# A two-layer transformer on one core: one more slot before layer 0's last mixing, sums at the ends of slots from there on, and a last block stored tile by tile

## The chip, the cores and the metric

The kernel runs on 1 core of a Trainium2 chip. The metric is the device time of one execution in microseconds (us). All matrix work is float32.

TensorE (PE) multiplies; its weight loads are shown as PEld. VectorE (DVE), ScalarE (ACT) and GpSimd (POOL) do the elementwise work, and SyncE (SP) issues nearly all DMAs. "PEclk" is the TensorE clock that was granted, as a share of full speed.

## The reference

The input `x` has 4 sequences of 512 positions with 256 features. Two transformer layers follow, each an attention and a feed-forward part behind a layer norm without parameters, with a residual add:

```
x = x + L0_attn(layernorm(x))   # 16 heads of 16, causal, softmax over up to 512 keys
x = x + L0_ffn(layernorm(x))    # per token AND output feature: softmax over 8 experts, the best two mixed
x = x + L1_attn(layernorm(x))   # 16 query heads of 128 on 4 key heads; attention over the 4 batch entries only
x = x + L1_ffn(layernorm(x))    # gated GELU, 256 -> 2048 -> 256, weights in 4 bits with scales
```

The feed-forward part of layer 0 is the one whose order matters here. For a token it computes 8 x 256 router logits and 8 x 256 expert results; for each of the 256 output features the two greatest of 8 logits choose two experts, their softmax weights are computed, all weights of one expert are summed over the 256 features, and the sums `c` (8 per token) mix the 8 expert results:

```
logits = (h @ router_w.T + router_b).reshape(T, O, E)
probs = softmax(logits); w, sel = top_k(probs, 2); w = w / sum(w)
c = zeros((T, E)).at[t_idx, sel].add(w)          # summed over the O features
final = einsum('te,teo->to', c, einsum('th,eoh->teo', h, expert_w) + expert_b)
```

## The kernel before

The 2048 tokens are 16 groups of 128 (the partitions), in 4 blocks of 4 groups. The residual stream `xres` stays in SBUF throughout. The order of instructions on PE, DVE, ACT and GpSimd is the order of the program, written out by hand.

**Layer 0's attention** is a loop over 44 batches `n` (block `j`, sequence `s`, head groups `gs`). A step issues the scores of the next batch (`greatest`, L652), subtracts this batch's maxima from the queries (`shift`, L681 and L684), adds the causal mask (`mask`, L665) and takes maxima (L671). Then follow a first `fill`, `mixed(n - 1)` (L736, the values times the exponentials, and their copy `avs`, L744), `powers(n)` (L700, the scores again; ACT's exponentials L709 into `pt`; GpSimd's causal zeroing L719) and a second `fill`. After the loop `mixed(43)` closes the layer.

**Slots.** `fill` is one slot of filler work. It counts `slot` up, gives PE and DVE a budget in us (what was overdrawn is carried over), and lets every `Stream` in `streams`, in order, emit its next piece while its engine has budget left and its condition holds. Streams are generators that yield `need(engine, cost, gap, cond)` before each piece; `gap` is a number of slots since the stream's piece before. The streams that matter here:

- `logit_pieces` (`lg`) and `result_pieces` (`eo`), the *products*: per group 4 router and 4 expert products of four matmuls each (L234), price 1.85. A product of logits needs the weights of two groups before; an expert product needs its group's weights, and its halves wait for earlier additions. ACT copies a logits product (L297), and multiplies an expert product by its two weights (L323, `part`).
- `weight_pieces`: DVE finds the two greatest of 8 (L371 to L397). ACT computes the lesser weight's tanh (`lesser`, L390, L391), two slots later. Then for each of 8 experts DVE writes a tile `owing` (L408, L426) and sums one part (L423), while ACT sums the other part from `owing` into `sums` (`sum_up`, L415). `total_pieces` (L436, L437) finishes the weights once all 8 sums are emitted.
- `addition_pieces` (L350 to L352): DVE adds four `part` tiles into `xres`.
- `divided(j, s)`: after a sequence's last mixing PE transposes `avs` (`av_T`, L754), DVE divides (L761, L762, `oq`), PE transposes back (`oq_T`, L771, only in an odd slot) and ACT copies that to `aT` (L774). After the last sequence of a block PE multiplies by `wo` in two steps (`o`, L783), each added to `xres` by DVE a slot or more later (L793).
- `norm_pieces`: a layer norm in pieces (statistics L180 and L181, `rs_v` L184, GpSimd's power L185, `xn` L194).

What `weight_pieces` hands to ACT isn't emitted at once. `defer(emit, slots, last)` puts it off by a slot (or two), and `emit_deferred` issues it either at the start of the slot where it is due, ahead of all streams, or at its end. For `sum_up` that is now decided by the slot in which it is put off:

```python
                defer(sum_up, last=slot % 2 == 1)
                yield need("DVE", 0.95, cond=lambda: len(deferred) < 6)
```

The PSUM pool `dn` has two tiles, which the products, `av_T`, `oq_T`, `o` and most projections take in turn.

**Layer 1's attention** loops over 16 head groups `p` (plus a first step for the projections of group 0): projections L987, scores L1000, softmax on DVE, values L1058, output L1078. Between its pieces `between` calls `fill` nine times a group, and what is left of layer 0's products is spread over the groups up to `LAST = 8`:

```python
            share = products_left / (9 * (LAST + 1 - p)) if p <= LAST else 0.0
```

with a PE budget of `1.9 * share + 0.2` and a DVE budget of `2.7 * share + 1.4` a slot. At `p == LAST + 2` a loop empties whatever is left before the last layer's weights are unpacked on DVE. Block 3's norm and transposes (`start_pieces(3)`) need the last addition of group 15 and must be done when `p == 11` begins.

**Layer 1's feed-forward part** computes gate and up (L916), the GELU on ACT and DVE, and `down` (L1234, `y`): per group 16 matmuls, then DVE's add into `xres` (L222). After the fourth group of a block one DMA on SP stores the block (L1239).

Of the kernel before, what the change touches and what calls it, by code (L numbers as in the profile page):

```python
# [21 lines left out]
NBLK = 4  # L22
# [10 lines left out]
def tile_transformer(  # L33
# [19 lines left out]
    nc = tc.nc  # L53
# [4 lines left out]
    xres = const.tile([P, NT, HID], F32, name="xres")  # L58

    def load_x(j):  # L60
        nc.sync.dma_start(
            out=xres[:, 4 * j : 4 * j + 4, :], in_=x[:, 4 * j : 4 * j + 4, :]
        )
# [48 lines left out]
    slot = 0  # L112

    def need(engine, cost, gap=0, cond=None):
        return engine, cost, gap, cond
# [21 lines left out]
    def defer(emit, slots=1, last=False):  # L137


        deferred.append((slot + slots, emit, last))  # L140

    def emit_deferred(last):
        for due in [d for d in deferred if d[0] <= slot and d[2] == last]:
            deferred.remove(due)
            due[1]()

    left = {"PE": 0.0, "DVE": 0.0}

    def fill(**budget):

        nonlocal slot
        slot += 1
        emit_deferred(False)
        for engine, b in budget.items():
            left[engine] = min(left[engine], 0.0) + b
        again = True
        while again:
            again = False
            for stream in list(streams):
                while stream.ready(left):  # L160
                    engine, cost = stream.go()
                    left[engine] -= cost
                    again = True
                if stream.next is None:
                    streams.remove(stream)
        emit_deferred(True)
# [188 lines left out]
    def weight_pieces():  # L355

        tt, stt = nc.vector.tensor_tensor, nc.vector.scalar_tensor_tensor
        lessers = []
        for g in range(NT):
            yield need("DVE", 1.25, cond=lambda: g in logits and logits[g][1] < slot)  # L360
            d = logits[g][0]
            hi4 = b1.tile([P, 4, HID], F32, tag="hi4", name=f"hi4_{g}")
            lo4 = b1.tile([P, 4, HID], F32, tag="lo4", name=f"lo4_{g}")
            m2 = b1.tile([P, HID], F32, tag="m2", name=f"m2_{g}")
            gap = b1.tile([P, HID], F32, tag="gap", name=f"gap_{g}")
            th = b1.tile([P, HID], F32, tag="th", name=f"th_{g}")
            w1 = b1.tile([P, HID], F32, tag="w1", name=f"w1_{g}")
            c1 = b5.tile([P, NE], F32, tag="c1", name=f"c1_{g}")
            sums = b5.tile([P, NE + 1], F32, tag="sums", name=f"sums_{g}")

            tt(hi4, d[:, 0:4], d[:, 4:8], ALU.max)  # L371
            yield need("DVE", 1.25)
            tt(lo4, d[:, 0:4], d[:, 4:8], ALU.min)
            yield need("DVE", 1.4)
            lo2, hi2 = lo4[:, 0:2], lo4[:, 2:4]
            tt(lo2, lo2, lo4[:, 2:4], ALU.max)
            tt(hi2, hi4[:, 0:2], hi4[:, 2:4], ALU.max)
            yield need("DVE", 1.4)
            tt(hi4[:, 0:2], hi4[:, 0:2], hi4[:, 2:4], ALU.min)
            tt(lo2, lo2, hi4[:, 0:2], ALU.max)  # L380
            yield need("DVE", 1.7)
            tt(gap, hi2[:, 0], hi2[:, 1], ALU.min)
            tt(m2, lo2[:, 0], lo2[:, 1], ALU.max)
            tt(m2, m2, gap, ALU.max)
            tt(gap, hi2[:, 0], hi2[:, 1], ALU.max)
            tt(gap, gap, m2, ALU.subtract)


            def lesser(th=th, gap=gap, w1=w1):
                nc.scalar.activation(th, gap, AF.Tanh, scale=0.5)  # L390
                nc.scalar.activation(w1, th, AF.Identity, bias=half_t, scale=0.5)  # L391
                lessers.append(th)

            defer(lesser, 2)
            for e in (0, 4):
                yield need("DVE", 1.25)
                tt(  # L397
                    d[:, e : e + 4], d[:, e : e + 4],
                    m2.unsqueeze(1).to_broadcast([P, 4, HID]), ALU.subtract,
                )  # L400

            yield need("DVE", 0.7, 1, cond=lambda: lessers)
            lessers.clear()
            owing = b5.tile([P, HID], F32, tag="owing", name=f"owing_{g}_")
            nc.vector.tensor_scalar(gap, gap, 0.0, -1.0, ALU.is_equal, ALU.mult)
            stt(owing, th, -1.0, gap, ALU.add, ALU.add)  # L408
            nc.vector.memset(sums[:, NE : NE + 1], 0.0)
            summed_up[g] = [c1, sums, 0]  # L410
            for e in range(NE):

                def sum_up(e=e, owing=owing, sums=sums, g=g):
                    spare = b2.tile([P, HID], BF16, tag="spare", name=f"spare_{g}_{e}")
                    nc.scalar.activation(  # L415
                        spare, owing, AF.Relu, scale=-1.0, accum_out=sums[:, e : e + 1]
                    )
                    summed_up[g][2] += 1

                defer(sum_up, last=slot % 2 == 1)  # L420
                yield need("DVE", 0.95, cond=lambda: len(deferred) < 6)
                junk = b2.tile([P, HID], BF16, tag="junk", name=f"junk_{g}_{e}")
                stt(junk, d[:, e], 0.0, w1, ALU.is_gt, ALU.mult, accum_out=c1[:, e : e + 1])  # L423
                if e < NE - 1:
                    less = b5.tile([P, HID], F32, tag="owing", name=f"owing_{g}_{e}")
                    stt(less, d[:, e], 0.0, owing, ALU.is_equal, ALU.add)  # L426
                    owing = less
            del logits[g]
# [20 lines left out]
    with ExitStack() as l0:  # L449
# [20 lines left out]
        def blank(j, i):  # L470
# [22 lines left out]
            out=later, in_=later, compare_op=ALU.is_ge, fill=NEG,  # L493
# [140 lines left out]
        for j in range(NBLK):  # L634
            n = (4, 2, 1, 1)[j]
            for s in range(NS):
                batches += [(j, s, range(g, g + n)) for g in range(0, 4, n)]
        NBT = len(batches)
# [194 lines left out]
        for n in range(NBT):  # L833
            j, s, gs = batches[n]
            if n in (1, 7):
                to = 2 if n == 1 else 3
                inputs[to] = Stream(prepare(to))
                streams.insert(0, inputs[to])
            if n + 1 < NBT and batches[n + 1][0] != j:
                while inputs[j + 1].next is not None:  # L840
                    fill(PE=2.0, DVE=2.0)
            with tc.high_priority(offset=AHEAD):
                if n + 1 < NBT:
                    greatest(n + 1)
                shift(n)
                if n + 1 < NBT:
                    mask(n + 1)

            fill(PE=(2.0, 2.0, 1.8, 1.6)[j], DVE=2.6)
            with tc.high_priority(offset=AHEAD):  # L850
                if n:
                    mixed(n - 1)
                powers(n)
            done += 1
            if n and batches[n - 1][2][-1] == 3:
                streams.insert(0, Stream(divided(*batches[n - 1][:2])))
            fill(PE=(2.4, 2.4, 2.2, 2.0)[j], DVE=2.6)
            if n < 4:
                w, dram = (rw, router_w) if n < 2 else (ew, expert_w)
                for i in range(4):  # L860
                    load_pair(w, dram, 4 * n % 8 + i)
                    loaded[n // 2, (4 * n % 8 + i) // 2] = slot
            for _ in range(1 + (n < 2) if blanked < 10 else 0):
                blank(2 + blanked // 5, (blanked + 4) % 5)
                blanked += 1
            if n in (0, 2):
                load_x(n // 2 + 2)
        mixed(NBT - 1)
        streams.insert(0, Stream(norm_pieces(0, b1, b2, normed_first)))
        last = Stream(divided(*batches[NBT - 1][:2]))  # L870
# [56 lines left out]
    with ExitStack() as l1:  # L927
# [3 lines left out]
        for kv, i in [(slice(None), slice(HPK + 1, HPK + 2))] + [  # L931
            (slice(kv, kv + 1), slice(0, HPK + 1)) for kv in range(NKV)
        ]:
            for hc in range(2):
                tc.keep_in_program_order(
                    nc.sync.dma_start(
                        out=wqkv[:, hc, kv, i], in_=w_qkv[hc * P : (hc + 1) * P, kv, i]
# [188 lines left out]
        for p in range(-1, NP):  # L1126
            j, kv = divmod(p, NKV)
# [54 lines left out]
    with ExitStack() as f1:  # L1182
# [47 lines left out]
        def down(j, it):  # L1230
            for t in range(4):
                ps = ps_o.tile([P, HID], F32, tag="o", name=f"y_{j}_{t}")
                for c in range(2 * NJ):
                    nc.tensor.matmul(  # L1234
                        ps, lhsT=it[:, c // 2, c % 2, t * P : (t + 1) * P],
                        rhs=wd[:, c // 2, c % 2, :], start=c == 0, stop=c == 2 * NJ - 1,
                    )
                add_residual(4 * j + t, ps)
            nc.sync.dma_start(  # L1239
                out=out[:, 4 * j : 4 * j + 4, :], in_=xres[:, 4 * j : 4 * j + 4, :]  # L1240
            )

        pending = None
        for j in range(NBLK):
# [62 lines left out]
```

## Time and profile before

| | |
|---|---|
| median of 3 runs | 1169.55 us (1169.44 to 1170.32) |
| the profiled execution | 1170.3 us, span 1168.6 us |
| granted TensorE clock in it | 1.000 |
| PE busy | 1142.0 us, 98% of the span |
| DVE busy | 809.8 us, 69% |
| ACT busy | 484.3 us, 41% |
| GpSimd busy | 108.4 us, 9% |
| waits of PE from 365 to 400 us (end of layer 0) | 4.1 us |
| waits of PE from 400 to 720 us (layer 1's attention beside layer 0's products) | 3.3 us |
| last store: issue | 1164.98 us |

The span runs from the first to the last instruction of one profiled execution; the time of an execution holds some more around it. Rows of the order of time read: start, duration, engine, line, operation, what is written from what, how many, and in brackets how long the engine had stood idle before and what released it. Rows of waits read: who waited for whom, the total, the times and the longest, in us. Rows by stretch read: the stretch and its length, then busy time and number of instructions of PE, PEld, DVE, ACT and POOL, the granted clock, the DMA engines' busy share and GB/s. Rows of DMA issues read: transfer, issuing queue, number, size of one and median us from issue to landing.

### The profile page before, as it was taken

Reading aid. Unit: us, or ns where it says so; the run is one execution under the profiler, and the core shown is the slowest. Engines: PE = TensorE matmul, PEld = TensorE weight load, DVE = VectorE, ACT = ScalarE, POOL = GpSimd, SP = SyncE. Lnnn points to the kernel's source line nnn. Section 1 sums busy time; section 2 is a strip of 40 time slices with the busy share of each in tenths; the row PEclk is TensorE's granted clock in tenths of the full one; section 3 lists DMA queues with packets and bytes.
Section 4 is the critical chain, followed back from the end, with each engine's and each line's share of the span. In section 5 each row is a group of like instructions: output and inputs, shape, how many; then the busy total and the mean of one; then the engine's idle time right before and its main releaser. Section 6 shows DMA issues by size and latency. Waiting matters only on the chain.

```text
span 1168.6 us, 18563 instructions
## 1 busy us (share of the span) xinstructions
PE 1142.0 (98%) x7178; PEld 661.5 (57%) x7178; DVE 809.8 (69%) x1783; ACT 484.3 (41%) x1099; POOL 108.4 (9%) x152
## 2 busy tenths in 40 slices
PE   7999999999999999999999999999999999999998
PEld 3666555556554445555555555566644475484487
DVE  5676889999988953868773785687699845716710
ACT  1444645556555542444443444544344312303300
POOL 7322221212112000000000000000000000000000
PEclk9999999999999999999999999999999999999999
DMA  7230110000000500000000001120110000000000
GB/s 219 64 83 2 19 20 2 2 1 2 2 2 1 181 1 1 1 1 1 1 1 1 1 1 46 28 54 21 27 46 1 0 1 19 0 1 19 1 18 19
DMA packets 21239, 26.46 MB, mean 23 GB/s; under 512 B 5128, under 2 KB 14600, under 8 KB 21152
## 3 DMA queue, kind: packets, MB, share of 16 engines
q1 hardware_dynamic: 20480, 24.10, 7.5%
q10 hardware_dynamic: 672, 1.18, 0.4%
q8 instruction: 56, 0.92, 0.3%
q14 instruction: 31, 0.25, 0.1%
HBM read 18.97 MB, written 2.10 MB: 18 GB/s over the span
## 4 chain that ended last, share of the span: by engine, by line
PE 81%; DVE 13%; ACT 2%; issue 1%; POOL 1%; DMA 0%; SPq 0%; ACTq 0%; DVEq 0%; POOLq 0%
PE qk_ps L987 11%; PE y L1234 9%; PE o L1078 9%; PE g L916 9%; PE u L916 9%; PE lg_ps L234 8%; PE eo L234 7%; PE s L652 3%; PE s L700 3%; DVE mx L671 3%; PE av L736 2%; PE v_ps L969 2%; PE qk_ps L545 2%; PE a L1058 1%; PE s L1000 1%
## 5 line engine op out<-in xcount | busy, mean ns | idle before, releaser
L987 PE MATMUL qk_ps<-xT,wqkv 128*128 128x512 f32 x320 | 148.9, 599 | 2.3 <-ACT part L323 1.2
L234 PE MATMUL lg_ps<-rw,xT 128*128 128x512 f32 x256 | 122.5, 601 | 1.4 <-ACT xT L954 0.3
L234 PE MATMUL eo<-ew,xT 128*128 128x512 f32 x256 | 121.5, 600 | 0.8 <-ACT lg L297 0.5
L1078 PE MATMUL o<-wpj,oT 128*128 128x256 f32 x512 | 119.1, 382 | 0.0
L1234 PE MATMUL y<-wd,it 128*128 128x256 f32 x512 | 111.8, 379 | 0.0
L1078 PEld LDWEIGHTS o<-wpj,oT 128*128 128x128 f32 x512 | 95.9, 190 | 27.5 <-issue 14.3
L1234 PEld LDWEIGHTS y<-wd,it 128*128 128x128 f32 x512 | 97.0, 190 | 15.0 <-issue 2.2
L671 DVE TENSOR_REDUCE mx<-s 128x1 f32<-128x384 f32 (+3 forms) x176 | 100.4, 632 | 1.3 <-PE s L665 1.3
L987 PEld LDWEIGHTS qk_ps<-xT,wqkv 128*128 128x128 f32 x320 | 59.1, 190 | 71.4 <-issue 57.4
L709 ACT ACTIVATE pt<-s 128x512 f32<-128x512 f32 (+1 forms) x176 | 84.1, 563 | 35.3 <-PE s L700 35.3
L916 PE MATMUL g<-xT,wgu 128*128 128x512 f32 x192 | 90.4, 593 | 0.0
L916 PE MATMUL u<-xT,wgu 128*128 128x512 f32 x192 | 90.2, 592 | 0.0
L323 ACT ACTIVATE part<-eo,c 128x256 f32<-128x256 f32 x128 | 53.7, 472 | 85.2 <-PE eo L234 75.2
L719 POOL TENSOR_SCALAR_AFFINE_SELECT pt<-pt 128x256 f32<-128x256 f32 (+2 forms) x88 | 63.2, 725 | 249.8 <-ACT pt L709 249.3
L1212 ACT ACTIVATE th<-sq 128x512 f32<-128x512 f32 x64 | 40.3, 630 | 87.6 <-DVE sq L1211 87.6
L234 PEld LDWEIGHTS lg_ps<-rw,xT 128*128 128x128 f32 x256 | 46.1, 190 | 46.1 <-issue 37.3
L234 PEld LDWEIGHTS eo<-ew,xT 128*128 128x128 f32 x256 | 46.1, 190 | 45.7 <-issue 38.3
L222 DVE TENSOR_TENSOR xres<-xres,y 128x256 f32<-128x256 f32 x16 | 6.7, 421 | 92.5 <-PE y L1234 92.5
L185 POOL TENSOR_TENSOR ln_rs<-rs_v,minus_half 128x4 f32<-128x4 f32 x16 | 17.6, 1099 | 552.2 <-DVE rs_v L184 439.9
L297 ACT COPY lg<-lg_ps 128x512 f32<-128x512 f32 x64 | 37.6, 588 | 73.5 <-PE lg_ps L234 73.5
L1213 DVE SCALAR_TENSOR_TENSOR th<-th,g 128x512 f32<-128x512 f32 x63 | 43.2, 686 | 29.2 <-ACT th L1212 29.2
L916 PEld LDWEIGHTS u<-xT,wgu 128*128 128x128 f32 x192 | 36.5, 190 | 45.9 <-issue 44.7
(233 smaller groups left out, 1776.8 us busy)
## 6 DMA issues: line engine op xcount, KB each, us to landing
qk<-stage SPq DMA_DIRECT2D x56, 64.0 KB, 2.4
wqkv<-in_w_qkv SPq DMA_DIRECT2D x8, 320.0 KB, 6.8
rw<-in_router_w SPq DMA_DIRECT2D x8, 256.0 KB, 7.8
ew<-in_expert_w SPq DMA_DIRECT2D x8, 256.0 KB, 4.6
wpj<-in_w_proj SPq DMA_DIRECT2D x1, 2048.0 KB
out<-xres SPq DMA_DIRECT2D x4, 512.0 KB, 2.6
xres<-in_x SPq DMA_DIRECT2D x3, 512.0 KB, 9.0
dq_wgu<-in_gate_w SPq DMA_DIRECT2D x8, 128.0 KB, 2.4
```

The costliest lines, as they stand in the source:

```text
L234: nc.tensor.matmul(ps, lhsT=xT[:, hc, (g % 4) * P : (g % 4 + 1) * P], rhs=w[:, hc, 2 * pair : 2 * pair + 2, :].rearrange("p e o -> p (e o) ...
L297: nc.scalar.copy(lg[:, 2 * pair : 2 * pair + 2, :].rearrange("p e o -> p (e o)"), ps)
L323: nc.scalar.mul(part[:, e % 4], ps[:, i], c[:, e : e + 1])
L671: nc.vector.tensor_reduce(maxes[n % 2][:, h, gs[0] : gs[0] + nb], ps[:, : nb * nk].rearrange("p (b k) -> p b k", b=nb), AX.X, ALU.max,)
L709: nc.scalar.activation(pt[:, i, : nb * nk], tiles[2 * pair + i][:, : nb * nk], AF.Exp, scale=0.25)
L719: nc.gpsimd.affine_select(out=last, in_=last, compare_op=ALU.is_ge, fill=0.0, base=0, pattern=pattern, channel_multiplier=-1,)
L916: nc.tensor.matmul(ps, lhsT=wgu[:, w, half, jj, par * P : (par + 1) * P], rhs=xT[:, half, :], start=half == 0, stop=half == 1,)
L987: nc.tensor.matmul(ps, lhsT=wqkv[:, hc, kv, h, :], rhs=xT[:, hc, :], start=hc == 0, stop=hc == 1,)
L1078: nc.tensor.matmul(ys[t // 2][:, t % 2], lhsT=state["o"][:, h, t * P : (t + 1) * P], rhs=wpj[:, HPK * kv + h, :], start=kv == 0 and h == 0 ...
L1212: nc.scalar.activation(th, sq, AF.Tanh, scale=0.7978845608028654)
L1213: nc.vector.scalar_tensor_tensor(th, th, 1.0, gp, ALU.add, ALU.mult)
L1234: nc.tensor.matmul(ps, lhsT=it[:, c // 2, c % 2, t * P : (t + 1) * P], rhs=wd[:, c // 2, c % 2, :], start=c == 0, stop=c == 2 * NJ - 1,)
```

## The change

There are three edits.

1. A flag `sums_last` takes the place of `slot % 2 == 1` in the `defer` of `sum_up`. In layer 0's loop it is true in the first slot of a step and false in the second, except for the last step; from there on it stays true, so every sum is issued at the end of its slot, behind what the streams emit.
2. One more slot, `fill(PE=2.0, DVE=1.2)`, is run between the loop and `mixed(43)`.
3. In the last block each group's tile (128 x 256, 128 KB) is stored by its own DMA after its add; the other blocks are still stored whole (512 KB).

```diff
     left = {"PE": 0.0, "DVE": 0.0}
+    sums_last = True
...
-                defer(sum_up, last=slot % 2 == 1)
+                defer(sum_up, last=sums_last)
...
+            sums_last = True
             fill(PE=(2.0, 2.0, 1.8, 1.6)[j], DVE=2.6)
             with tc.high_priority(offset=AHEAD):
                 if n:
...
+            sums_last = n == NBT - 1
             fill(PE=(2.4, 2.4, 2.2, 2.0)[j], DVE=2.6)
...
+        fill(PE=2.0, DVE=1.2)
         mixed(NBT - 1)
         streams.insert(0, Stream(norm_pieces(0, b1, b2, normed_first)))
         last = Stream(divided(*batches[NBT - 1][:2]))
         streams.insert(0, last)
         while last.next is not None:
             fill(PE=2.0, DVE=2.6)
...
                 add_residual(4 * j + t, ps)
-            nc.sync.dma_start(
-                out=out[:, 4 * j : 4 * j + 4, :], in_=xres[:, 4 * j : 4 * j + 4, :]
-            )
+                if j == NBLK - 1 or t == 3:
+                    of = slice(4 * j + (t if j == NBLK - 1 else 0), 4 * j + t + 1)
+                    nc.sync.dma_start(out=out[:, of, :], in_=xres[:, of, :])
```

## The prediction

> **What bounds the kernel now.** First the page, for the busy shares and the span; then the busy time by stretches; then the order of time around the end of layer 0, which the change touches, on TensorE (PE), ScalarE (ACT) and VectorE (DVE); last the end of the program.
>
> ```profile
> span 1168.6 us, 18563 instructions
> PE 1142.0 (98%) x7178; PEld 661.5 (57%) x7178; DVE 809.8 (69%) x1783; ACT 484.3 (41%) x1099; POOL 108.4 (9%) x152
> ...
> 350.00:400.00 50.00, 45.43 (x344) 24.05 (x343) 44.59 (x115) 27.60 (x79) 7.60 (x9) 1.00 0.18 60
> 400.00:450.00 50.00, 48.59 (x219) 23.89 (x218) 27.85 (x83) 23.25 (x56) 2.33 (x2) 1.00 0.15 47
> ```
>
> PE is busy for 1142.0 of 1168.6 us. The 26.6 us left are what a reordering can win, and most are out of reach: 8.6 lie in the first 30 us and 4.5 after 1150. The stretch 350 to 400 holds 4.57 us of idle PE (50 - 45.43), more than any other between. There the last mixing of layer 0 stands:
>
> ```profile
> 372.89 1.21 PE L736 MATMUL av<-pt,va 128*32 128x128 f32 x28
> 374.89 0.41 PE L736 MATMUL av<-pt,va 128*32 128x128 f32 x4 [0.79 <-POOL pt L719]
> 375.23 0.76 PE L754 MATMUL av_T<-ident,avs 128*128 128x128 f32 x4
> 375.83 1.88 PE L234 MATMUL lg_ps<-rw,xT 128*128 128x512 f32 x4
> 377.55 0.38 PE L771 MATMUL oq_T<-ident,oq 128*128 128x128 f32 x2
> 378.39 1.98 PE L234 MATMUL eo<-ew,xT 128*128 128x512 f32 x4 [0.46 <-ACT lg L297]
> 382.12 1.99 PE L783 MATMUL o<-wo,aT 128*128 128x256 f32 x8 [1.74 <-ACT aT L774]
> 383.95 1.88 PE L234 MATMUL eo<-ew,xT 128*128 128x512 f32 x4
> 385.94 1.98 PE L234 MATMUL lg_ps<-rw,xT 128*128 128x512 f32 x4
> 387.76 1.89 PE L783 MATMUL o<-wo,aT 128*128 128x256 f32 x8
> ```
>
> The brackets are PE's idle time before that row and what ended it: 0.79 us for GpSimd's causal mask of the last `pt`, 0.46 for a PSUM tile of the pool `dn`, 1.74 for `aT`. Together 2.99 us. Why `aT` was late is on ACT and DVE:
>
> ```profile
> 376.03 0.26 DVE L761 RECIPROCAL rden<-av_T 128x16 f32<-128x16 f32 x1 [1.47 <-PE av_T L754]
> ...
> 381.30 0.42 ACT L415 ACTIVATE spare<-owing__4607 128x256 bf16<-128x256 f32 x1 [2.96 <-DVE owing__4607 L408]
> ...
> 381.71 0.35 ACT L774 COPY aT<-oq_T 128x256 f32<-128x256 f32 x1
> ...
> 385.20 0.68 DVE L793 TENSOR_TENSOR xres<-xres,o 128x512 f32<-128x512 f32 x1
> ```
>
> `oq_T` was done at about 377.9, but ACT stood 2.96 us before a sum of a weight (`sum_up`, L415) whose `owing` DVE had not yet written; the copy to `aT` was queued behind it. It is a sum that is emitted at a slot's start.
>
> **The change, part by part.** The sum is made against the profiled execution: 1170.3 us, with a span of 1168.6 and 1.7 around it. The median of the runs is 1169.55, 0.75 lower; the difference is carried over.
>
> Sums inside layer 0: nothing moves. In PE's order `oq_T` (which asks for an odd slot) always follows the mask matmuls L665, so first slots of a step are odd and second ones even, through all 44 steps; the new flag then gives the same start or end as `slot % 2` did. Value 0.
>
> The added slot. Call the second slot of step 43 S0, and the next ones S1, S2 and so on. Before: `mixed(43)`; S1 `av_T` and one logits product; S2 nothing on PE, since no product was ready; S3 `oq_T` (odd) and an expert product; S4 `o` and a product. After: S1 a product; `mixed(43)`; S2 `av_T`; S3 `oq_T`. So the slot adds no work: the product of 375.83 goes ahead of the mixing, and `oq_T` keeps its slot. A product takes 1.73 us (four matmuls at about 0.43 apart), from about 372.8 to 374.5; the mask that was awaited was done at 374.84, and the 28 matmuls that don't need it take until 375.5. The 0.79 is gone. The lesser's two activations (0.42 + 0.51) move ahead of `avs` on ACT and are done near 374.9, before `avs` is wanted. On DVE the 1.2 of budget lets one addition (L350 to L352, 0.68 + 0.43 + 0.43 = 1.5 us) run where DVE idled 1.47; the first norm's statistics go one slot later, and its `xn` is not read before 392.92, 10 us after it was written. No DMA is issued in these slots; SP's next, the loads of `wqkv` at 389.68, follows the end of the second `o` (389.65) and moves with it, as do the values that first read it at 394.51.
>
> What is late next: `oq`. With `av` done at 375.8, `av_T` at 376.5 and DVE's 0.26 + 0.42, `oq` is there at about 377.3. If the addition made an expert product ready in S2, it covers that; if not PE waits 0.7. Then `dn` with its two tiles: if S2 and S3 both hold expert products, the second waits about 0.5 for ACT's two multiplications (0.84). I charge 0.6.
>
> Sums at the end. The first two sums now come behind `aT` and the `part` copies of their slot. The copy runs at about 379, `o` at 379.4 to 380.9 instead of 382.12: the 1.74 goes, and the 0.46 with it. Next behind it is the residual add L793, whose PSUM tile PE needs again: by the budgets two or three weight steps fewer (0.69 each) stand ahead of it, and one addition (1.5) may come in between, so it ends at 383.5 to 384.8, not 385.88. The second `o` then starts at about 384.8 after as many products as before; it was 387.76. So this place gives 2.99 - 0.6 = 2.4 us.
>
> In layer 1 the same ACT work is done (128 rows of L415 after 401 in all, activation and read, 0.41 + 0.19 a pair) but half the sums come up to one slot later. PE idles there 3.3 us between 400 and 720, and the largest piece (1.2, `qk_ps` behind `part`) hangs on a DVE addition, not on a sum. The trace has no run of the other order: I bound this part by -1.0 (a third of those waits, the ones with ACT ahead, vanish) and +1.0 (as much again appears), and take 0. The cover is slack: 252 of the 512 rows of L234 lie after 401, so some 64 of 128 products are spread over 90 slots, and a group's eight last 11 slots; DVE's pieces of a group, 18.1 us as the code prices them and 3.1 of additions, need 21.2 / (2.7 x 64/90 + 1.4) = 6.4 slots of budget.
>
> The stores. The last block's store waits for the last tile:
>
> ```profile
> 1164.98 0.33 SPq L1239 DMA_DIRECT2D out<-xres  x1
> ...
> dq_wgu<-in_gate_w SPq DMA_DIRECT2D x8, 128.0 KB, 2.4
> ...
> out<-xres SPq DMA_DIRECT2D x4, 512.0 KB, 2.6
> ```
>
> After, 128 KB follow the last add instead of 512. Three more issues (0.34 each) stand on SP, which has nothing else, 6.9 us apart, beside PE. The landing: 2.4 by the row of that size (2.1 for `dq_wd`), a gain of 0.2 to 0.5; by the rate of the old store, 400 GB/s in its middle, 0.39 MB less are 1.0 us. [...] The trace has 6.9 us between tiles for each 2.6, so only the last counts. I take 0.6, and keep 0.2 to 1.0.
>
> Sum: -2.4 + 0 - 0.6 = -3.0. 1170.3 - 3.0 = 1167.3 for the profiled kind of execution, 1169.55 - 3.0 = 1166.5 for the median.
>
> **Rivals.** *A wait takes the place.* DVE is busy 44.6 of 50 us in that stretch. If the residual add stays behind the same pieces, the second `o` is held by its PSUM tile and only 0.79 and the stores remain: -0.8 - 0.6 = -1.4, 1168.2. For it: PE's weight load before 385.94 was already waiting on L793. Against: the addition fills DVE's own 1.47 us of idle time. Chance 0.15.
>
> *The sums come too late at the end of the products* (slower). The last group's total and products were these:
>
> ```profile
> 691.29 0.17 DVE L436 TENSOR_TENSOR sums<-sums 128x8 f32<-128x8 f32 x1 [0.48 <-ACT spare L415]
> ...
> 699.84 3.60 PE L234 MATMUL eo<-ew,xT 128*128 128x512 f32 x8
> ```
>
> The next head group starts at 703.27, and from there `share` is 0 and a slot's PE budget 0.2: one product a group. One slot (3.4 us) later, one or two products slip there, and the last to the loop at `LAST + 2` (721). This delays block 3's norm (DVE at 705.87) by some 18 us, and its transposes from 723-729 to 735-740, still ahead of 743, where PE must have them. One slot costs nothing. Decisive is more than one: each group's logits wait for the weights two groups before, so over groups 8 to 15 the delay can add up four times, 14 us, if the slots have no slack. Then PE stands at that loop through the eight steps of the last weights (0.69 each, 5.5) and their sums and addition (3): -3.0 + 8.5 gives 1175. Against: the slack above. Chance 0.14.
>
> *The change doesn't act*: `fill` finds no product in S1. Then only the sums (1.74) and the store (0.6) act: -2.3, 1167.2. Against: one was ready at 375.83 under the same conditions. Chance 0.03.
>
> **How the numbers follow.** 0.2% of 1169.55 is 2.3 us, about what a measurement of this kernel can tell from no change; faster means under 1167.2. The forecast has 0.68; its own range is -2.4 ± 0.6 for the place, ± 1.0 for layer 1 and +0.4 to -0.4 for the store, 1164.8 to 1168.2, and 0.04 of it is counted above 1167.2. Faster is then 0.64; same is 0.04 + 0.15 + 0.03 = 0.22; slower 0.14. The range 1164.8 to 1169.6 holds all but the slower case and the forecast's lowest end.
>
> **What would show it.** Right: a product's four matmuls stand before the last L736 with no wait for `pt`; L774 comes ahead of the first L415 after it; `o` starts within 2 us of `oq_T`; PE's idle time from 350 to 400 falls from 4.57 to about 2.2; the last issue is followed by under 2.5 us. L234 still ends before the group at 721 begins. Wrong: a wait of PE on L793 or L774 of over 1 us, products after 721, or idle PE between 400 and 745 of over 5 us.

## The result, and the profile after

The changed kernel takes 1171.73 us (median of 21 runs, 1169.88 to 1173.22), the kernel before in runs beside it 1170.17 us (21 runs, 1169.03 to 1170.85). The ratio is 1.0013, with a 95% interval of 1.0007 to 1.0019: slower by 1.6 us. That is less than the 2.3 us of the prediction's bound, but clear of no change, opposite to the forecast, and 2.1 us above the upper end of the range. The profiled execution took 1171.34 us, with a span of 1169.6.

Line numbers of the changed kernel are 1 higher than before up to the residual add of layer 0, and 5 higher in layer 1: L234 is L235, `aT` L775, `o` L784, the add L794, `qk_ps` L992, the stores L1246.

The page:

```profile
span 1169.6 us, 18569 instructions
PE 1142.3 (98%) x7178; PEld 662.4 (57%) x7178; DVE 809.1 (69%) x1783; ACT 482.3 (41%) x1099; POOL 108.6 (9%) x152
```

Busy time by stretches (stretch, length, PE, PEld, DVE, ACT, POOL, granted clock, DMA share, GB/s):

```profile
350.00:400.00 50.00, 45.82 (x347) 24.60 (x346) 45.64 (x115) 28.03 (x79) 7.24 (x9) 1.00 0.23 76
400.00:450.00 50.00, 47.84 (x216) 23.45 (x215) 29.31 (x83) 22.79 (x56) 2.01 (x2) 1.00 0.10 31
700.00:750.00 50.00, 46.67 (x260) 27.92 (x259) 25.98 (x62) 17.64 (x32) 2.85 (x2) 0.97 0.10 28
```

From 350 to 400 PE idles 4.18 us where it idled 4.57. The surprise is the third row: 3.33 us of idle time from 700 to 750, and a clock of 0.97, where before had 1.000 throughout. No edit stands there.

Following the same operations through both profiles shows where it turns. Each number is the start in the changed kernel against the start before:

| operation | before | after | lead |
|---|---|---|---|
| second `o` of layer 0's end | 387.76 | 385.23 | -2.53 |
| first `v_ps` of layer 1 | 394.51 | 393.50 | -1.01 |
| values `a` of head group p = 10 | 725.79 | 723.58 | -2.21 |
| values `a` of head group p = 11 | 752.46 | 754.72 | +2.26 |
| first gate product | 823.52 | 825.41 | +1.89 |
| span | 1168.6 | 1169.6 | +1.0 |

So 2.5 us are won where the prediction saw them, and 1.5 of them are gone at the first `v_ps`. At p = 10 the lead is 2.2, of which 0.6 is a set of transposes that the kernel before has done by then and the changed one has not. Then 4.5 are lost in a single head group, 340 us behind the place. At the first gate product the kernel is 1.9 behind, and the last store gives 0.9 back.

**The end of layer 0**, PE, ACT and DVE in order of time:

```profile
372.74 1.88 PE L235 MATMUL lg_ps<-rw,xT 128*128 128x512 f32 x4
374.55 1.08 PE L737 MATMUL av<-pt,va 128*32 128x128 f32 x32
377.15 0.44 PE L772 MATMUL oq_T<-ident,oq 128*128 128x128 f32 x2 [0.81 <-DVE oq L763]
379.15 1.89 PE L784 MATMUL o<-wo,aT 128*128 128x256 f32 x8
383.41 1.98 PE L235 MATMUL eo<-ew,xT 128*128 128x512 f32 x4 [0.65 <-DVE xres L794]
385.23 1.89 PE L784 MATMUL o<-wo,aT 128*128 128x256 f32 x8
391.68 1.98 PE L235 MATMUL lg_ps<-rw,xT 128*128 128x512 f32 x4 [1.34 <-ACT xT L959]
...
377.63 0.37 ACT L775 COPY aT<-oq_T 128x256 f32<-128x256 f32 x1 [1.67 <-PE oq_T L772]
383.27 0.42 ACT L416 ACTIVATE spare<-owing__4611 128x256 bf16<-128x256 f32 x1
390.64 0.42 ACT L416 ACTIVATE spare<-owing 128x256 bf16<-128x256 f32 x1 [0.17 <-DVE owing L427]
391.06 1.05 ACT L959 COPY xT<-xT_ps 128x512 f32<-128x512 f32 x2
```

The mixing stands behind a product and no longer waits for `pt`; the copy to `aT` comes 5.6 us ahead of the first sum; `o` starts 2.0 us after `oq_T`. New are the waits of 0.81 for `oq`, 0.65 for the residual add, and 1.34 for layer 1's `xT`, whose copies stand on ACT behind three sums (the third is shown).

**The loss**, in order of time: PE, SP's queue, DVE, ACT.

```profile
718.34 1.88 PE L235 MATMUL eo<-ew,xT 128*128 128x512 f32 x4
731.40 0.66 PE L211 MATMUL xT_ps<-ident,xn 128*128 128x128 f32 x4 [3.01 <-ACT qT L996]
732.37 3.56 PE L992 MATMUL qk_ps<-xT,wqkv 128*128 128x512 f32 x4 [0.32 <-ACT qT L996]
...
721.16 0.33 SPq L888 DMA_DIRECT2D dq_wgu<-in_gate_w  x1
721.54 3.67 SPq L890 DMA_DIRECT2D dq_sgu<-in_gate_s  x8
725.25 0.42 SPq L888 DMA_DIRECT2D dq_wgu<-in_up_w  x1
...
727.87 0.43 DVE L900 TENSOR_SCALAR dq_mgu<-dq_wgu 128x512 int32<-128x512 int32 x1 [2.79 <-DMA dq_wgu<-in_up_w]
...
728.75 1.15 ACT L902 ACTIVATE dq_bgu<-dq_mgu,minus 128x1024 f32<-128x1024 int32 x1 [4.48 <-DVE dq_mgu L901]
730.75 0.60 ACT L996 COPY qT<-qk_ps 128x512 f32<-128x512 f32 x1
```

Read it from the top. The very last expert product of layer 0 runs at 718.34, in the loop at `LAST + 2`; before, it stood in the run of eight matmuls at 699.84. SP's loads of layer 1's packed weights use the SBUF that layer 0 held, and in both profiles the first one is released by ACT's last `part` (after a wait of SP of 12.6 us before, of 31.4 after), so they start only then. Before, the same load and the first instruction that uses the two loads stood here:

```profile
704.37 0.34 SPq L883 DMA_DIRECT2D dq_wgu<-in_gate_w  x1
...
721.28 0.38 DVE L895 TENSOR_SCALAR dq_mgu<-dq_wgu 128x512 int32<-128x512 int32 x1
```

The load stood 16.8 us earlier, 16.9 us ahead of DVE's unpacking. As before, the second packed load stands behind eight small loads of scales (3.67 us of issue), and now it lands only at about 727.8. Behind that one landing three engines stand in line: DVE idles 2.79 us before it unpacks, ACT 4.48 us before its part of the unpacking (L902), and the copy to `qT` behind that on ACT holds the PSUM that PE's transposes need: 3.01 us.

Behind the idle time the granted clock falls. PE alone (stretch, length, busy, granted clock, DMA share, GB/s):

```profile
731.00:734.00 3.00, 2.28 (x6) 0.70 0.23 58
734.00:737.00 3.00, 3.00 (x9) 0.74 0.24 71
```

The clock is halved once, from about 732.2 to 735.6 (0.50 from 732.3 to 735.5), and four `qk_ps` matmuls take 3.56 us where four took 1.98. PE between the values of p = 10 and those of p = 11, before and after:

```profile
725.79:752.46 26.67, 26.40 (x141) 1.00 0.06 17
723.58:754.72 31.14, 27.81 (x142) 0.95 0.17 45
```

PE idles 3.33 us instead of 0.27, and the halved clock makes it busy for 1.4 us longer. Together that is the whole 4.5.

**The last store** (transfer, queue, number, size, median us from issue to landing):

```profile
out<-xres SPq DMA_DIRECT2D x3, 512.0 KB, 2.6
out<-xres SPq DMA_DIRECT2D x4, 128.0 KB, 1.7
```

Each issue took 0.33 to 0.37 us and nothing waited for it.

### The profile page after: what moved, and what is told of

It reads as the page before. It is cut to its first block, busy times and chain, and to the rows that moved or that the text cites. A ratio compares the mean times of both kernels' runs of the same rounds, so it can differ in the third digit from the quotient of the medians.

```text
span 1169.6 us, 18569 instructions
## 1 busy us (share of the span) xinstructions
PE 1142.3 (98%) x7178; PEld 662.4 (57%) x7178; DVE 809.1 (69%) x1783; ACT 482.3 (41%) x1099; POOL 108.6 (9%) x152
## 4 chain that ended last, share of the span: by engine, by line
PE 82%; DVE 12%; ACT 1%; issue 1%; POOL 1%; DMA 1%; SPq 1%; ACTq 0%; DVEq 0%; POOLq 0%
PE qk_ps L992 11%; PE y L1239 9%; PE o L1083 9%; PE g L921 9%; PE u L921 9%; PE lg_ps L235 8%; PE eo L235 8%; PE s L653 3%; PE s L701 3%; DVE mx L672 3%; PE v_ps L974 2%; PE av L737 2%; PE qk_ps L546 2%; PE a L1063 1%; PE s L1005 1%
## 5 line engine op out<-in xcount | busy, mean ns | idle before, releaser
L992 PE MATMUL qk_ps<-xT,wqkv 128*128 128x512 f32 x320 | 150.0, 603 | 0.6 <-ACT qT L996 0.6
L235 PE MATMUL eo<-ew,xT 128*128 128x512 f32 x256 | 122.2, 600 | 3.1 <-ACT xT L279 1.4
L235 PE MATMUL lg_ps<-rw,xT 128*128 128x512 f32 x256 | 122.4, 601 | 2.2 <-ACT xT L959 1.3
L992 PEld LDWEIGHTS qk_ps<-xT,wqkv 128*128 128x128 f32 x320 | 59.8, 191 | 70.2 <-issue 60.1
L235 PEld LDWEIGHTS lg_ps<-rw,xT 128*128 128x128 f32 x256 | 46.2, 190 | 46.9 <-issue 37.5
L235 PEld LDWEIGHTS eo<-ew,xT 128*128 128x128 f32 x256 | 46.1, 190 | 46.2 <-issue 35.9
```

The costliest lines, as they stand in the source:

```text
L235: nc.tensor.matmul(ps, lhsT=xT[:, hc, (g % 4) * P : (g % 4 + 1) * P], rhs=w[:, hc, 2 * pair : 2 * pair + 2, :].rearrange("p e o -> p (e o) ...
L992: nc.tensor.matmul(ps, lhsT=wqkv[:, hc, kv, h, :], rhs=xT[:, hc, :], start=hc == 0, stop=hc == 1,)
```

## The experiments

Three theories of the loss. **A**: the late last product holds back SP's loads, and DVE, ACT and PE stand in line behind the second packed load. **B**: the late product holds back block 3's norm, by way of the last addition, and with it the transposes. **C**: sums at the ends of slots let many small waits appear between 400 and 720. Below, ratios are against runs of the kernel before on the same chip (medians 1169.82, 1169.89 and 1170.09 in three groups).

### The store alone (`e1_store`, before with the third edit only)

> The kernel before with the tile-by-tile stores of the last block alone. The stores are worth what their landing shows (1.7 us in the changed kernel against 2.6 before): 0.9 us faster than before, with PE's order and waits as before. The other theory, that the end is set by something else than the landing (three more DMAs to complete), gives no difference within 0.2 us, or slower.

1169.32 us, ratio 0.9995 (0.9987 to 1.0003). The landing is 1.7 again. The median is 0.5 us lower, not 0.9, and the timed runs can't tell that from nothing.

### Both packed loads ahead of the scales (`e2_packed_first`)

```diff
         for i in range(2):
             nc.sync.dma_start(out=wi[:, i], in_=packed[i])
+        for i in range(2):
             for b in range(8):
                 nc.sync.dma_start(out=sc[16 * b : 16 * b + 16, i], in_=scales[i](b))
```

> The changed kernel with both loads of packed weights issued ahead of the 16 loads of scales; the late last product of layer 0 stays. Theory A (the loads of packed weights, let go only by that product, stand in SP's queue, and DVE, ACT and PE wait in their order behind the unpacking): the second load is issued 4 us earlier, at about 721.5 instead of 725.25, DVE's 2.8 us before L900, ACT's 4.5 before L902 and PE's 3.0 before the first transpose of block 3 fall to under 1, the TensorE clock stays at 1.00 there, and the time falls by about 4.5 us below the changed kernel, to 2.5 to 3 us below the kernel before. Theory B (PE waits there because block 3's norm comes late): PE's wait stays at 2 us or more, time within 1 us of the changed kernel. Theory C (the loss is spread over layer 1 by the sums at the slots' ends): the same, within 1 us.

1169.13 us, ratio 0.9995 (0.9987 to 1.0003), 2.6 below the changed kernel. SP and PE in order of time:

```profile
722.04 0.43 SPq L888 DMA_DIRECT2D dq_wgu<-in_up_w  x1
...
729.05 0.65 PE L211 MATMUL xT_ps<-ident,xn 128*128 128x128 f32 x4 [0.17 <-ACT qT L997]
730.02 1.98 PE L993 MATMUL qk_ps<-xT,wqkv 128*128 128x512 f32 x4 [0.32 <-ACT qT L997]
```

The product is as late as before this edit, but the second packed load is issued 3.2 us earlier, and both the wait of 3.01 and the halved clock are gone. This edit moves one link of theory A alone. Only 2.6 of the expected 4.5 us came back; waits of `g` for `th` in the feed-forward part rose from 0.5 to 2.2 us, about as much as is missing.

### The share kept above zero (`e3_share`, repeated as `e3_repeat`)

```diff
-            share = products_left / (9 * (LAST + 1 - p)) if p <= LAST else 0.0
+            share = products_left / (9 * max(LAST + 1 - p, 1))
```

> The changed kernel with a PE budget in the head group after LAST as well, so that layer 0's last product runs some 11 us earlier and not in the loop at LAST + 2. Theory A: the loads of packed weights start at about 710 and nothing waits for them, the clock stays at 1.00: 4 to 5 us below the changed kernel, 2.5 to 3.5 below the kernel before. Theory B (late norm of block 3): the same gain. Theory C (the sums at the slots' ends cost throughout layer 1): within 1 us of the changed kernel.

1165.01 us, ratio 0.9962 (0.9949 to 0.9974).

```profile
705.66 1.88 PE L235 MATMUL eo<-ew,xT 128*128 128x512 f32 x4
...
708.48 0.34 SPq L888 DMA_DIRECT2D dq_wgu<-in_gate_w  x1
```

A product that is left after p = 8 is now given a slot in p = 9 instead of waiting for the loop. It runs 12.7 us earlier, SP's loads follow it by as much, and PE has no wait at all from 718 to 760. This is the first link of A, and its median is 6.7 us below the changed kernel's, more than the expected 4 to 5 (in `e3_repeat` below it is 5.3). In the kernel before no product is left after p = 8, so by the code this rule alone changes nothing there.

> The changed kernel with the PE budget after LAST once more, on the same chip as the two others, for the comparison: 1165.0 as before.

On another chip: 1166.46 us, 0.9968 (0.9956 to 0.998). The two profiles of this same kernel part before any edited place: a mixing at 367.69 in the one starts at 368.85 in the other. The profiles of this study fall into two patterns there (this row starts at 367.6 to 368.0, or at 368.7 to 369.3), so differences of that size between single profiles mean nothing. The profiles of the kernel before and of the changed one share the later pattern (368.86 and 368.80), so the table above compares like with like.

### The unpacking held back (`e7_hold`)

```diff
-        yield need("DVE", 0.9)
+        yield need("DVE", 0.9, hold)    # hold = 8 slots for the first piece of the first quarter, else 0
```

> The changed kernel with the first unpacking of weights held back by 8 slots; the late product and the late loads stay as they are. Theory A: the transposes of block 3 no longer have an unpacking ahead of them on DVE and ACT; PE's 3.0 us wait and the slow clock go, about 4 us below the changed kernel, unless the later unpacking is then awaited at the first gate and up products. Theory B: the wait stays, within 1 us of the changed kernel.

1167.59 us, ratio 0.998 (0.9974 to 0.9987). The last product stays at 717.56, and block 3's norm hangs on it as in the changed kernel. Yet the transposes have no wait:

```profile
717.56 1.88 PE L235 MATMUL eo<-ew,xT 128*128 128x512 f32 x4
727.45 0.60 PE L211 MATMUL xT_ps<-ident,xn 128*128 128x128 f32 x4
```

So B falls: with the last addition as late as in the changed kernel the transposes wait for nothing, and the loss lay in the unpacking that stood in front of them. A wait of 1.4 of `a` for `pT` came instead, which leaves it behind `e3_share`.

### One slot alone, the flag alone (`e4_slot`, `e5_sums`)

Before with `fill(PE=2.0, DVE=1.2)` only, and before with `sums_last` only.

> The kernel before with the added slot alone (sums by the slot's parity, whole stores). In its order one product of layer 0 again runs only in the loop at LAST + 2, and the copy to aT already stands ahead of the first sum. Theory A (the late product brings a loss of 4 to 5 us, whichever edit made it late; the place at the end of layer 0 gains 2 to 2.5): PE waits 2 to 3 us before block 3's first transpose, 1.5 to 3 us slower than the kernel before. Theory C (the loss comes from the sums at the slots' ends in layer 1): no such wait, 2 us faster than before.

1172.89 us, ratio 1.0032 (1.002 to 1.0044). Its seven runs spread from 1171.2 to 1176.0, three of them near 1175.9; the profile is of a run of 1171.2 and doesn't show what those three add.

> The kernel before with the sums at the slots' ends alone (no added slot, whole stores). One product again runs in the loop at LAST + 2. Theory A: the wait before block 3's transposes is there as well; aT is no longer late (1.74 gained at the end of layer 0, the 0.79 for pt stays), 2 to 3.5 us slower than before. Theory C: slower too, but with the loss spread over PE's waits from 400 to 720, which rise from 3.3 to over 5 us.

1170.91 us, ratio 1.0008 (1.0 to 1.0016), 1.0 us slower than before where 2 to 3.5 was expected. The same row in each, the slot first:

```profile
730.91 1.11 PE L210 MATMUL xT_ps<-ident,xn 128*128 128x128 f32 x4 [3.06 <-ACT qT L992]
```

```profile
730.40 0.66 PE L211 MATMUL xT_ps<-ident,xn 128*128 128x128 f32 x4 [3.02 <-ACT qT L994]
```

Either edit alone springs the trap. And with the flag alone PE's waits from 400 to 720 are 2.2 us, fewer than before's 3.3: C falls. In both, `aT` is no longer late: a slot puts the first sum off as well as the flag does.

### Each edit with the share kept above zero (`e4_slot_share`, `e5_sums_share`)

> The kernel before with the added slot, and a PE budget in the head group after LAST (which is without effect in the kernel before, whose products are done by then). Theory A: the trap is gone, and what the slot is worth is left: 2 to 3 us faster than before. Theory C: the same as the slot alone, since no sum moved.

A miss: 1171.45 us, ratio 1.0007 (0.9999 to 1.0014). The trap at 731 is gone, but another wait is left, which `e4_slot` has too (2.14 us at 403). ACT and PE in order of time:

```profile
401.54 0.42 ACT L415 ACTIVATE spare<-owing__4789 128x256 bf16<-128x256 f32 x1 [1.50 <-DVE sums L409]
402.24 0.42 ACT L415 ACTIVATE spare<-owing 128x256 bf16<-128x256 f32 x1 [0.18 <-DVE owing L426]
404.07 0.57 ACT L974 COPY v<-v_ps 128x512 f32<-128x512 f32 x1
...
404.69 5.40 PE L988 MATMUL qk_ps<-xT,wqkv 128*128 128x512 f32 x8 [2.15 <-ACT v L974]
```

With sums still at the starts of some slots, four of them stand on ACT ahead of a copy to `v` and wait for DVE. Eight matmuls took 5.40 us at a lower clock (0.66 from 404 to 408); in `e4_slot`, at a clock of 1.00 there, the same eight took 3.70. Its 13 runs fall into two groups: six from 1168.94 to 1169.45 with a mean clock of 0.999 or more, seven from 1171.45 to 1173.12, nearly all at 0.997 or 0.998.

> The kernel before with the sums at the slots' ends and a PE budget in the head group after LAST. Theory A: the trap is gone; 1 to 2 us faster than before (aT's 1.74, less what the sums do ahead of the first xT copies of layer 1, about 1.3). Theory C: still slower than before, since the sums at the ends cost in layer 1.

1165.36 us, ratio 0.996 (0.9947 to 0.9972), more than I had expected. The flag by itself is worth most of the gain once the products don't slip: PE's waits from 400 to 760 are 2.2 us instead of before's 4.4.

### Without the slot, and with sums later (`e8_no_slot`, `e9_later`)

The first is the changed kernel with the share above zero and without the added slot. The second keeps the slot and puts the sums off by two slots between the end of layer 0 and the first inputs of layer 1:

```diff
-                defer(sum_up, last=sums_last)
+                defer(sum_up, sums_slots, last=sums_last)   # 2 in that stretch, else 1
```

> Sums at the slots' ends, a PE budget in the head group after LAST and the stores tile by tile, but no added slot. If the slot is worth what the prediction charged for it beyond the sums (0.79 for pt), this is 0.5 to 1 us slower than the same kernel with the slot (1165.0). If the wait for oq has taken the place of the wait for pt, both take the same time within 0.5 us.

1164.92 us (1164.77 to 1165.10), ratio 0.9956 (0.9944 to 0.9969). Beside it `e3_repeat`, which differs from it in the slot alone and has the same first pattern, took 1.5 us more. PE's longest waits from 380 to 700 (who for whom, total, times, longest), without the slot:

```profile
PE lg_ps L235 <- ACT part L324: 0.9, 1, 0.9
PE qk_ps L990 <- ACT v L976: 0.8, 1, 0.8
```

and with it:

```profile
PE eo L235 <- ACT xT L279: 1.4, 1, 1.4
PE lg_ps L235 <- ACT xT L959: 1.3, 1, 1.3
```

The slot trades the 0.8 us for `pt` for 0.8 for `oq`, and brings two longer waits for `xT` behind it. With it the second `o` starts 1.3 us earlier (385.28 against 386.54), but the first `v_ps` 0.3 later (393.55 against 393.24). Neither of the two expectations, slower without it or the same, was right. That the slot costs time is shown on this chip only: the runs of `e3_share`, the same kernel as `e3_repeat` on another chip, took 1164.64 to 1165.84.

> The changed kernel with the PE budget after LAST, and the sums put off by one slot more between the end of layer 0 and layer 1's first values, so that two of them no longer stand ahead of the first copies to layer 1's xT. If ACT's wait for those sums is what keeps PE from the product behind the transposes (1.3 us), that wait falls under 0.5 and the time by about 1 us, to 1164. If not, no difference within 0.5 us.

1163.94 us (1163.40 to 1164.78), ratio 0.9948 (0.9936 to 0.9961), 2.5 us below `e3_repeat`. The wait for layer 1's `xT` is down from 1.34, though not under the expected 0.5, and the other wait for `xT`, of 1.4, is gone:

```profile
389.96 7.13 PE L975 MATMUL v_ps<-wqkv,xT 128*128 128x512 f32 x16 [0.85 <-ACT xT L960]
```

It has the lowest median of all, 0.5% below the kernel before; that it beats `e8_no_slot` isn't shown, since the intervals overlap.

## Why the prediction was wrong

**The place at layer 0's end: right.** Predicted -2.4 at the second `o`, measured -2.53. The waits for `pt`, the PSUM tile and `aT` went; for what would be late next 0.6 was charged, and 0.81 for `oq` and 0.65 for the residual add came. But a part was given back at once: the first `v_ps` leads by only 1.0, because PE waits 1.34 us there for the `xT` copies, which stand on ACT behind three sums. (In `e5_sums`, without the slot, that wait isn't there.) PE's idle time from 350 to 400 was to fall to 2.2 us and stands at 4.18. The sum had followed the path to the second `o` and stopped there, so this term was 1.4 too large where layer 1 begins. (Of the 4.5 us that it counts idle after 1150, 0.4 lie behind the span's end; nothing rests on that.) And the two edits aren't worth their own share of it: in `e4_slot` and `e5_sums` the 1.74 for `aT` goes with either.

**The stores: right in the landing.** It fell from 2.6 to 1.7 us, and the span's end gained 0.9 where 0.6 was charged; in timed runs (`e1_store`) the gain isn't clear of nothing.

**Layer 1 at 0: the step that failed.** The sum put this term at 0 ± 1.0, and one head group of it cost 4.5. "The cover is slack" and "One slot costs nothing" are the words. The rival "The sums come too late at the end of the products" had the place: the last product did slip to the loop at `LAST + 2`. It then asked one question, whether block 3's norm would still be in time, and answered it rightly, as `e7_hold` shows. What it overlooked is that the last product frees SBUF. SP's loads of the packed weights hang on it, and what DVE and ACT unpack from them stands in the engines' fixed order ahead of copies that PE needs. Before's profile held the clue in one row: SP's first packed load at 704.37, just after the last product's end at 703.4, with its data used at 721.28. The cover was 17 us, and a slip to the loop takes it all.

**The cause of the slip was wrong too.** The rival looked for late sums, and its slack was counted for DVE's pieces alone (6.4 of 11 slots). In the changed kernel the last total of the weights comes at 689.26, 2.0 us earlier than before's 691.29. What differs is the PE budget. More products were done ahead of p = 8, so that 6 were left there instead of 8. The share fell from 8/9 to 6/9, and a slot's budget from 1.89 to 1.9 x 0.67 + 0.2 = 1.47. A product's price is 1.85: with 1.89 a rest of 0.04 is left, and a second product goes in the same slot; with 1.47 none is left. The last group's four products, before and after:

```profile
692.95 3.60 PE L234 MATMUL eo<-ew,xT 128*128 128x512 f32 x8
...
699.84 3.60 PE L234 MATMUL eo<-ew,xT 128*128 128x512 f32 x8
```

```profile
691.74 1.88 PE L235 MATMUL eo<-ew,xT 128*128 128x512 f32 x4
...
695.18 1.88 PE L235 MATMUL eo<-ew,xT 128*128 128x512 f32 x4
...
700.34 1.88 PE L235 MATMUL eo<-ew,xT 128*128 128x512 f32 x4
```

Before, they go in two pairs, with a slot between them for the addition that the second pair waits for. After, one by one, two miss the group: from p = 9 a slot's budget is 0.2, which lets one more go at 700.34 and the last only in the loop, at 718.34. This is worked out from the code and the rows; no run changed the share at p = 8 alone. `e3_share` changes only the budget after p = 8, and with it +1.6 turns into -4.8 (-3.6 in `e3_repeat`). Being ahead of the plan made the kernel late.

**The price.** The rival gave 1175 with "more than one" slot as its point of decision; one product was enough, for +4.5 us at p = 10, a third of it by the clock, which no step priced. The range ended at 1169.6 because it priced that case by the norm alone, at nothing. Of the signs named, the wait over 1 us on L793 or L774 didn't come; idle time of over 5 us from 400 to 745 did: 6.6, where before had 4.0.

## What to carry to other kernels

When a filler's last piece may move, list everything that its end releases, buffers and the DMA queue behind them included, and follow each release through the engines' fixed order to the one that sets the time; the first dependent found is not the only one. A budget that is spread over what is left shrinks when work runs ahead, so leave no stage in which it is zero while a piece may remain. A load that a whole line of engines will wait for goes ahead of its small companions in the queue: in this case eight of them took 3.67 us to issue, and `e2_packed_first` came out 2.6 us below the changed kernel.

## What the runs showed of the hardware that was not expected

A wait of PE of 3.0 us cost about 4.6 in the changed kernel: 3.01 idle, and 1.58 more for four matmuls at the halved clock. Three profiles have such a wait at 731 (3.01 in the changed kernel, 3.06 in `e4_slot`, 3.02 in `e5_sums`), and all three have a lower clock there, 0.83 from 730 to 740; the ten profiles without the wait have 1.00. The slow rows don't begin at the same place: in the changed kernel the clock falls 0.8 us after PE resumes; in `e4_slot` the four transposes that PE resumes with take 1.11 us already, where the other two have 0.66; in `e5_sums` the eight `o` matmuls behind the `qk_ps` are slow too, 2.30 us against 1.89. The wait of 2.15 us in the profile of `e4_slot_share` was followed by a lower clock as well (0.66 from 404 to 408), the one of 2.14 us in `e4_slot` at the same place was not (1.00).

A run's mean clock doesn't show which stretch was halved: it is under 1.000 in all 21 runs of the changed kernel, all 7 of `e4_slot` and all 13 of `e5_sums`, but also in 11 of 41 of the kernel before. In the profile of `e5_sums_share` it is 0.999, with 1.00 in every stretch up to 1150 and 0.93 from 1150 on. And in five profiles the clock falls once before 200 us: it is 0.83 from 190 to 200 in `e3_share`, `e4_slot`, `e7_hold` and `e9_later`, where PE is busy for all 10 us (0.50 from 192 to 194 in `e3_share` and `e7_hold`), and 0.99 from 60 to 200 in `e1_store`. These five are the profiles of the earlier of the two patterns of the first 370 us. Why the clock falls there, and what a wait must be for it to fall behind it, the runs don't show.
